# Moving the stores of the normalised tiles to GpSimd's queue, the shared weights' loads to a later place, and the transposes and half chunks around the last tile

## The chip, the cores and the metric

The kernel runs on one core of one Trainium2 chip. The metric is the device time of one execution in microseconds (us), taken as the median of three runs. The engines are named as in the profile: PE is TensorE (matmuls, with weight loads as PEld), DVE is VectorE, ACT is ScalarE, POOL is GpSimd, SP is SyncE. SP, ACT and POOL can each issue DMAs from a queue of their own. [...]

## The reference, cut to what matters

One transformer block with adaptive layer norm, over 2048 tokens of width 512, all in 32-bit floats: attention with 16 heads of 128, then a mixture of 64 experts of hidden size 128 with the best 4 per token, beside 2 shared experts of hidden size 512.

```python
h = _layernorm(x) * (1 + ca) + sa
x = x + ga * attention(h)                        # 16 heads, causal, output projection O_w
h = _layernorm(x) * (1 + cb) + sb
scores = softmax(h @ Wr + router_bias)           # 64 experts
topk_scores, topk_idx = top_k(scores, 4)
pos = running count of each expert's tokens      # valid where pos < 128
xb[eid, pos] = h[tok]
yb = (silu(xb @ Wg) * (xb @ Wu)) @ Wd            # each expert
out = sum over a token's 4 experts of w * yb
hs = silu(h @ Sg) * (h @ Su)                     # 2 shared experts
out = out + hs @ Sd
x = x + gb * out
```

## The kernel before

The tokens lie in 16 tiles of 128 rows, 4 tiles to a block of 512. The program has four stages. In all of them the order of the work is written out by hand (inside `manual_schedule`), by lists of closures and by tables that say behind which matmul of which tile something is emitted. Around these hand-written orders the compiler may still interleave the instructions of one stage with those of the next, where they are independent.

**Attention** (lines 188 to 670) ends with the last head's values. Its last lines store the attention of each head and pair of tiles to `atd` from GpSimd's queue (L489).

**Output projection with the router** (L873 to L938). For each tile `t` from 4 to 15, 16 matmuls (one for each head, index `hd`) of 128x512 build `pso` (L915) from the pair buffer `abs_[t // 2]`, which `load_ab` loads from `atd` on SP's queue (L544), and `wo`. At the end of a tile VectorE adds it to `acc` (L936) and `norm(t)` (L728 to L744) makes the normalised tile: statistics on VectorE, a square root on ScalarE (L735), then `h` on VectorE (L738, L741, L742), and a store of `h` to `h2d` in DRAM from SP's queue (L743). `h` has 4 buffers, so that `norm(t + 4)` needs the store of tile `t` to be finished. Tiles 0 to 3 were begun earlier and are finished at L899 to L908.

Between the 16 matmuls of a tile, four tables place the router's work of earlier tiles. The key is (tile, index of the matmul behind which it is emitted), the value is the tile or block concerned:

- `TURN`: `turn_h` transposes `h` of a tile on TensorE (`tp`, L749), and ScalarE copies it to `h2T` (L750).
- `LOGIT`: `logit` multiplies it with the router's weights (`pl`, L758). After every second tile `choose` (L766 to L807) follows on VectorE and ScalarE: softmax, best four, one-hot masks.
- `POSITION`: `positions` (L809 to L850) counts the seats on TensorE (`pos`, L819) and works out the seats on VectorE (L824 to L848). `pos` and `pl` share one PSUM bank.
- `SEAT`: `seat_tokens` (L852 to L871) collects the table of tokens per expert (L859). After the last block it gives `tok`, the list by which GpSimd gathers the experts' rows.

The loads of the next stage's shared weights, `wsg` and `wsu` (two of 1 MB each, L895 and L896), are issued on SP's queue at the head of this stage, behind the loads of `x`.

**Lead of the shared experts** (L1141 to L1178). `shared_up(b, i)` gives two half chunks: four matmuls with `wsg` and four with `wsu` (`psg`, L978), each of 128x512; after the second, `glu` makes `hs`: a sigmoid on ScalarE (L966) and two multiplications on VectorE (L967, L968). `psg` has three PSUM buffers. `LEAD = 8` half chunks are computed in this plain way, and the router's work of the last tile is placed between them, by their number `n`: the transpose of tile 15, its logits and `choose`, the positions and the seats of the last block. `wsd`, the shared experts' output weights, is loaded here (L1155) and multiplied by `gb` on GpSimd (L1157), eight instructions of 128x512. `token_sum` prepares sums of tokens on VectorE for the next stage.

**Experts and shared units** (L1183 to L1257). For every expert GpSimd gathers 128 rows of `h2d` by `tok` (L1190), TensorE transposes them (`tpx`, L1200) and runs the expert (`pse` L1207, `tph` L1222, `psy` L1228). `merge` interleaves this with the rest of the shared work. A shared unit does what two half chunks do with 7 products of half the size instead of 8 (Strassen's scheme: `first` to `fourth`, `pst`, L1062), that is 14 matmuls of 128x256, with sums on VectorE. `shared_down` (`psd`, L1122) multiplies `hs` by `wsd`. A **tail** (L1259 to L1299) gathers the experts' rows for every token, adds them and stores the result.

Of the kernel before, what the change touches and what calls it, by code (L numbers as in the profile page):

```python
# [18 lines left out]
P = 128  # L19
# [4 lines left out]
def adaln_block_kernel(  # L24
# [23 lines left out]
    nc = tc.nc  # L48
# [3 lines left out]
    S, _, HS = Sg.shape  # L52
# [5 lines left out]
    NHC = S * HS // P  # L58
# [3 lines left out]
    NP = NT // 2  # L62
# [15 lines left out]
    gb = const.tile([P, D], F32)  # L78
    atd = dram.tile([H, DH, N], F32)
    h2d = dram.tile([N, D], F32)  # L80
# [43 lines left out]
    with ExitStack() as att:  # L124
# [63 lines left out]
        with tc.tile_pool(name="pre", bufs=1) as pre, tc.manual_schedule():  # L188
# [4 lines left out]
            for b in range(NB):  # L193
                xb = pre.tile([P, 4, D], F32, name="xb", bufs=NB)
                nc.sync.dma_start(
                    out=xb, in_=x[0, b * 512 : (b + 1) * 512, :].rearrange("(i p) d -> p i d", p=P)
                )
                xs.append(xb)
                if b == 0:
                    wms = {}  # L200
                    for i in (1, 0):
                        wms[i] = pre.tile([P, DC, D], F32, name="wm", bufs=2)
                        nc.sync.dma_start(
                            out=wms[i],
# [334 lines left out]
        def load_ab(pr, dst=None, heads=((0, 4), (4, 8), (8, 12), (12, 15))):  # L539

            if pr not in abs_:
                abs_[pr] = vp.tile([P, H, 2 * P], F32, name="v") if dst is None else dst
            for a, b in heads:
                nc.sync.dma_start(  # L544
                    out=abs_[pr][:, a:b, :],
                    in_=atd[a:b, :, pr * 256 : (pr + 1) * 256].rearrange("h p t -> p h t"),
                )
# [130 lines left out]
    wsg = shw.tile([P, S, DC, HS], F32)  # L678
    wsu = shw.tile([P, S, DC, HS], F32)
# [48 lines left out]
    def norm(t):  # L728

        st = rt.tile([P, 6], F32, name="st", bufs=3)  # L730
        nc.vector.bn_stats(st, acc[:, t, :])
        mv = rt.tile([P, 2], F32, name="mv", bufs=3)
        nc.vector.bn_aggr(mv, st)
        rstd = rt.tile([P, 1], F32, name="rstd", bufs=3)
        nc.scalar.activation(rstd, mv[:, 1:2], AF.Sqrt, bias=eps, scale=1.0)  # L735
        nc.vector.reciprocal(rstd, rstd)
        h = rt.tile([P, D], F32, name="h", bufs=4)
        nc.vector.tensor_scalar(  # L738
            h, acc[:, t, :], mv[:, 0:1], rstd, ALU.subtract, ALU.mult
        )  # L740
        nc.vector.tensor_mul(h, h, cb)  # L741
        nc.vector.tensor_add(h, h, sb)  # L742
        nc.sync.dma_start(out=h2d[t * P : (t + 1) * P, :], in_=h)  # L743
        hs_[t] = h  # L744

    def turn_h(t):
# [131 lines left out]
    POSITION = {(5, 14): 0, (6, 10): 1}  # L878
    SEAT = {(6, 5): 0, (7, 0): 1}
    for t in range(7, NT):  # L880
        TURN[t, 7] = t - 1
        LOGIT[t, 12] = t - 1
        if t - 2 in LASTS:
            POSITION[t, 7] = LASTS.index(t - 2)
        if t - 3 in LASTS and t > 7:
            SEAT[t, 3] = LASTS.index(t - 3)
    with tc.manual_schedule():
        load_x(1)
        load_ab(3, heads=ALL)
        load_ab(2, heads=((15, 16),))  # L890
        route_consts()
        for j in range(2, NB):
            load_x(j)
        for s in range(S):
            nc.sync.dma_start(out=wsg[:, s], in_=Sg[s].rearrange("(k p) h -> p k h", p=P))  # L895
            nc.sync.dma_start(out=wsu[:, s], in_=Su[s].rearrange("(k p) h -> p k h", p=P))  # L896
        for t in range(NE):
            ps = psO.tile([P, D], F32, name="pso", tag="y")
            nc.tensor.matmul(  # L899
                out=ps,  # L900
                lhsT=last3[:, t * P : (t + 1) * P] if t < NE - 1 else ones,
                rhs=wo[:, H - 1, :],
                start=True,
                stop=True,
            )
            nc.vector.tensor_add(acc[:, t, :], parts[t], ps)
        for t in range(NE):
            norm(t)  # L908
        for t in range(NE, NT):
            pr, i = divmod(t, 2)  # L910
            if i == 0 and 3 <= pr < NP - 1:
                load_ab(pr + 1, heads=ALL)
            ps = psO.tile([P, D], F32, name="pso", tag="y")
            for hd in range(H):
                nc.tensor.matmul(  # L915
                    out=ps,
                    lhsT=abs_[pr][:, hd, i * P : (i + 1) * P],
                    rhs=wo[:, hd, :],
                    start=(hd == 0),
                    stop=(hd == H - 1),  # L920
                )
                if hd == 5:
                    nc.vector.tensor_add(acc[:, t, :], acc[:, t, :], ga)
                if (t, hd) in TURN:
                    turn_h(TURN[t, hd])
                if (t, hd) in POSITION:
                    positions(POSITION[t, hd])
                if (t, hd) in SEAT:
                    seat_tokens(SEAT[t, hd])
                if (t, hd) in LOGIT:  # L930
                    u = LOGIT[t, hd]
                    logit(u)
                    if u in LASTS:
                        for _ in choose(LASTS.index(u)):
                            pass
            nc.vector.tensor_add(acc[:, t, :], acc[:, t, :], ps)  # L936
            norm(t)
# [3 lines left out]
    with ExitStack() as ex:  # L941
# [154 lines left out]

        def fourth(n):
            u = units[n]
            (p2,) = products(n, (2,))
            nc.vector.tensor_add(u["g"][:, :HB], u["p1"], p2)  # L1100
            sig = sgp.tile([P, 512], F32, name="sig512")
            nc.scalar.activation(sig, u["g"], AF.Sigmoid)
            b, i = UNITS[n]
            hsh[b, i] = hsp.tile([P, 512], F32, name="hs")

            def finish():
                nc.vector.tensor_mul(sig, sig, u["g"])
                nc.vector.tensor_mul(hsh[b, i], sig, u["up"])

            glus.append(finish)  # L1110
            if b + 2 < NB:
                for j in {4: (1, 2), 5: (3,), 6: (4,)}.get(i, ()):
                    token_sum(b + 1, j)
            if n + 1 == len(UNITS):
                glus.pop()()
            del units[n]
# [17 lines left out]
            nc.sync.dma_start(out=out[0, t * P : (t + 1) * P, :], in_=acc[:, t, :])  # L1134


        LEAD = 8
        shared = []
        for i in range(LEAD // 2):
            shared += shared_up(0, i)  # L1140
# [12 lines left out]

        with tc.manual_schedule():
            nc.sync.dma_start(out=wsd, in_=Sd.rearrange("s (i p) d -> p (s i) d", p=P))  # L1155
            for i in range(NHC):
                nc.gpsimd.tensor_mul(wsd[:, i, :], wsd[:, i, :], gb)  # L1157
            for e in range(3):
                load_up(e)
                load_down(e)  # L1160
            for n, (_, f) in enumerate(shared[:LEAD]):
                f()
                if n == 0:
                    turn_h(NT - 1)
                if n == 1:
                    seat_tokens(len(BLOCKS) - 2)
                if n == 1:
                    logit(NT - 1)
                    choice = choose(len(BLOCKS) - 1)
                    next(choice)  # L1170
                if n == 2:
                    next(choice)
                if n == 4:
                    positions(len(BLOCKS) - 1)
                if n == 6:
                    seat_tokens(len(BLOCKS) - 1)
                if n >= 4:
                    token_sum(0, n - 3)  # L1178
        rts.close()
        tsp = ex.enter_context(tc.tile_pool(name="tsp", bufs=1))  # L1180
        wsp = ex.enter_context(tc.tile_pool(name="wsp", bufs=1))
# [163 lines left out]
```

## Time and profile before

| what | us |
|---|---|
| runs of the kernel before | 2517.18, 2517.94, 2519.73 |
| their median | 2517.94 |
| the profiled execution, device time | 2528.37 |
| its span in the trace | 2526.5 |
| TensorE busy in that span | 2427.2 |
| output projection and router, about | 1772 to 1983 |
| lead of the shared experts, about | 1983 to 2021 |
| experts and shared units, about | 2021 to 2400 |
| tail, about | 2400 to 2527 |

The profile is of one execution, and its times are counted from the start of the span. A line of the timeline has the start, the duration, the engine, the line of the kernel, the operation, what is written and read, the shapes and the count; a bracket at its end gives how long the engine had been idle before it, and what released it. Matmuls overlap, so their durations count some time twice: the distance between starts is what a group costs. A 32-bit matmul of 128x512 has two records in the trace. The granted clock of TensorE is given as a share of the full clock. A wait for several things is put down to the one that came last.

### The profile page before, as it was taken

To read this page: it belongs to the slowest core of one execution; us is meant where nothing else is said; L and a number is where in the kernel's file an instruction comes from. 1 tells how busy PE (TensorE), PEld (TensorE's weight loads), DVE (VectorE), ACT (ScalarE), POOL (GpSimd) and SP (SyncE) were. 2 spreads that over 40 slices of the span, in tenths; PEclk is the share of its full clock that TensorE was granted. 3 is DMA by queue.
4 is the path that set the end of the run, shared out by engine and by line. 5 is a ranking of instruction groups with operands and counts; after the bars stand their busy time and mean duration, and the time that the engine had idled before them with its cause. 6 is when DMAs were issued, how large, how long until landed. Compare 5 with 4: busy or idle time off the path is not lost.

```text
span 2526.5 us, 26293 instructions
## 1 busy us (share of the span) xinstructions
PE 2427.2 (96%) x8537; PEld 1529.5 (61%) x8537; DVE 1518.9 (60%) x2969; ACT 655.7 (26%) x1476; POOL 250.9 (10%) x306
## 2 busy tenths in 40 slices
PE   7999999999999999999999999979999899999989
PEld 4666666666666666666666666545444486877733
DVE  4566666666666666666666666664655552654645
ACT  3223323333333332323333223311111121222200
POOL 0000000000000000000000000040000211111173
PEclk9999999999999999999999999989999999999999
DMA  4234434444454444443444444574612376877564
GB/s 138 61 92 105 116 91 108 111 99 110 96 122 105 101 119 101 98 118 89 110 111 104 110 99 113 130 215 133 215 54 75 92 208 209 247 219 232 176 202 127
DMA packets 225423, 326.25 MB, mean 129 GB/s; under 512 B 32100, under 2 KB 140680, under 8 KB 225288
## 3 DMA queue, kind: packets, MB, share of 16 engines
q1 hardware_dynamic: 197960, 251.16, 38.5%
q0 software_dynamic: 18112, 56.64, 7.5%
q10 hardware_dynamic: 9216, 16.78, 1.8%
q8 instruction: 69, 1.13, 0.2%
q14 instruction: 66, 0.54, 0.1%
HBM read 139.91 MB, written 41.94 MB: 72 GB/s over the span
## 4 chain that ended last, share of the span: by engine, by line
PE 64%; DVE 19%; SPq 6%; issue 4%; DMA 4%; ACT 2%; another core or an unknown queue 0%; DVEq 0%; ACTq 0%; POOL 0%; POOLq 0%
PE pqk L169 12%; PE ps L408 11%; PE po L479 9%; DVE pt L461 7%; SPq L451 6%; PE pv L329 5%; PE pst L1062 5%; PE pso L915 4%; PE psd L1122 4%; PE pse L1207 4%; DVE nm L421 4%; DMA pt<-p 3%; PE psg L978 3%; DVE p L397 3%; PE psy L1228 2%
## 5 line engine op out<-in xcount | busy, mean ns | idle before, releaser
L427 ACT ACTIVATE p<-ps,nm 128x1024 f32<-128x1024 f32 (+7 forms) x384 | 331.9, 864 | 1042.3 <-DVE nm L425 369.7
L408 PE MATMUL ps<-kt,qt 128*128 128x512 f32 (+3 forms) x1280 | 535.7, 535 | 45.8 <-ACT p L427 45.0
L479 PE MATMUL po<-pt,v 128*128 128x256 f32 (+1 forms) x2304 | 567.0, 368 | 6.5 <-DVE pt L461 3.6
L479 PEld LDWEIGHTS po<-pt,v 128*128 128x128 f32 x2304 | 425.7, 190 | 221.0 <-issue 156.1
L421 DVE TENSOR_REDUCE nm<-ps 128x1 f32<-128x1024 f32 (+7 forms) x384 | 349.6, 910 | 91.2 <-PE ps L408 82.4
L461 DVE STREAM_TRANSPOSE pt<-pt 128x1664 f32<-128x1664 f32 (+2 forms) x160 | 318.0, 1988 | 66.2 <-DMA pt<-p 61.6
L408 PEld LDWEIGHTS ps<-kt,qt 128*128 128x128 f32 x1280 | 235.4, 191 | 196.7 <-issue 127.1
L420 DVE TENSOR_TENSOR ps<-ps,causal 128x128 f32<-128x128 f32 x256 | 74.4, 291 | 347.7 <-PE ps L408 347.7
L489 POOL DMA_DIRECT2D atd<-at x128 | 78.2, 612 | 1650.7 <-ACT at L488 1626.2
L329 PE MATMUL pv<-wv,hT 128*128 128x256 f32 x1024 | 240.3, 379 | 0.0
L169 PE MATMUL pqk<-hT,wk 128*128 128x512 f32 x512 | 233.0, 598 | 0.0
L169 PE MATMUL pqk<-hT,wq 128*128 128x512 f32 x512 | 230.0, 592 | 0.0
L397 DVE TENSOR_SCALAR p<-p,rs 128x1024 f32<-128x1024 f32 (+7 forms) x384 | 221.7, 605 | 9.3 <-DMA p<-atd 0.2
L329 PEld LDWEIGHTS pv<-wv,hT 128*128 128x128 f32 x1024 | 194.5, 190 | 31.4 <-issue 1.9
L915 PE MATMUL pso<-hT,v 128*128 128x512 f32 x384 | 175.6, 604 | 0.0
L169 PEld LDWEIGHTS pqk<-hT,wk 128*128 128x128 f32 x512 | 98.2, 192 | 103.3 <-issue 100.9
L169 PEld LDWEIGHTS pqk<-hT,wq 128*128 128x128 f32 x512 | 97.2, 190 | 96.4 <-issue 93.3
L1207 PE MATMUL pse<-wgu,xbT 128*128 128x256 f32 x512 | 121.1, 379 | 0.0
L915 PEld LDWEIGHTS pso<-hT,v 128*128 128x128 f32 x384 | 70.7, 192 | 74.5 <-issue 73.5
L1122 PE MATMUL psd<-wsd,hs 128*128 128x512 f32 x256 | 111.5, 592 | 0.0
L1207 PEld LDWEIGHTS pse<-wgu,xbT 128*128 128x128 f32 x512 | 94.0, 190 | 12.3 <-issue 1.4
L1190 POOL DMA_INDIRECT xb<-h2d,tok x64 | 65.0, 1016 | 293.9 <-PE tpx L1200 279.9
(263 smaller groups left out, 1956.7 us busy)
## 6 DMA issues: line engine op xcount, KB each, us to landing
pt<-p SPq DMA_DIRECT2D x768, 104.0 KB
pt<-p SPq DMA_DIRECT2D x256, 124.0 KB
pt<-p SPq DMA_DIRECT2D x256, 108.0 KB
atd<-at POOLq DMA_DIRECT2D x128, 128.0 KB
wgu<-in_L_ffn_Wg_dram SPq DMA_DIRECT2D x64, 256.0 KB
wgu<-in_L_ffn_Wu_dram SPq DMA_DIRECT2D x64, 256.0 KB
wd<-in_L_ffn_Wd_dram SPq DMA_DIRECT2D x64, 256.0 KB
ybd<-y ACTq DMA_DIRECT2D x64, 256.0 KB
```

The lines of the kernel that those rows point to most:

```text
L169: nc.tensor.matmul(out=ps, lhsT=w[:, k, :], rhs=hT[:, k, j * 512 : (j + 1) * 512], start=(k == 0), stop=(k == DC - 1),)
L329: nc.tensor.matmul(out=ps, lhsT=hT[:, k, t * P : (t + 1) * P], rhs=wv[:, k].rearrange("p i d -> p (i d)"), start=(k == 0), stop=(k == DC - 1),
L397: nc.vector.tensor_scalar(cols[:, :, a:b], cols[:, :, a:b], rs[:, n : n + 1], None, ALU.mult)
L408: nc.tensor.matmul(out=ps[:, o : o + wo], lhsT=q, rhs=kts[hd, (c0 + o) // 512][:, :wo], start=True, stop=True,)
L421: nc.vector.tensor_reduce(nm[:, n : n + 1], ps[:, :w], AX.X, ALU.max, negate=True)
L427: nc.scalar.activation(rows[:, r0 + c0 // P : r0 + (c0 + w) // P], ps[:, :w].rearrange("q (r b k) -> q r b k", b=4, k=32), AF.Exp, bias=nm ...
L451: nc.sync.dma_start(out=pt[32 * b : 32 * (b + 1), a * w : (a + 1) * w], in_=pb[32 * a : 32 * (a + 1), b * w : (b + 1) * w],)
L461: nc.vector.transpose(part, part)
L479: nc.tensor.matmul(out=po if wide else po[:, P:], lhsT=vts[g][:, kt, hh * DH : (hh + 1) * DH], rhs=rows[:, r : r + last + 1 : last] if wid ...
L915: nc.tensor.matmul(out=ps, lhsT=abs_[pr][:, hd, i * P : (i + 1) * P], rhs=wo[:, hd, :], start=(hd == 0), stop=(hd == H - 1),)
L1122: nc.tensor.matmul(out=ps, lhsT=hsh[b, f][:, i * P : (i + 1) * P], rhs=wsd[:, f, :], start=(f == 0), stop=(f == NHC - 1),)
L1207: nc.tensor.matmul(out=ps, lhsT=xts[e][:, k, :], rhs=weights[e][:, k].rearrange("p i h -> p (i h)"), start=(k == 0), stop=(k == DC - 1),)
```

## The change

It has five parts. The store of the normalised tile goes from SP's queue to GpSimd's. The loads of `wsg` and `wsu` go from the head of the output stage to tile 11 (the first shared expert) and tile 13 (the second), behind the load of the pair buffer. For tiles 7 to 15 the transpose of the tile before is emitted after matmul 10 instead of 7, and the logits after matmul 14 instead of 12. `LEAD` goes from 8 to 10 half chunks, and the work placed between the half chunks comes one half chunk later, so that one more half chunk stands ahead of the last tile's transpose and two follow the last seats. The multiplication of `wsd` by `gb` goes from GpSimd to VectorE, three instructions, three and two in the fourth step of the first three shared units; two of the later `token_sum` calls come one unit later.

```diff
@@ norm
-        nc.sync.dma_start(out=h2d[t * P : (t + 1) * P, :], in_=h)
+        nc.gpsimd.dma_start(out=h2d[t * P : (t + 1) * P, :], in_=h)
@@ tables
     for t in range(7, NT):
-        TURN[t, 7] = t - 1
-        LOGIT[t, 12] = t - 1
+        TURN[t, 10] = t - 1
+        LOGIT[t, 14] = t - 1
@@ output stage
-        for s in range(S):
-            nc.sync.dma_start(out=wsg[:, s], in_=Sg[s].rearrange("(k p) h -> p k h", p=P))
-            nc.sync.dma_start(out=wsu[:, s], in_=Su[s].rearrange("(k p) h -> p k h", p=P))
...
             if i == 0 and 3 <= pr < NP - 1:
                 load_ab(pr + 1, heads=ALL)
+            if i == 1 and pr >= NP - 1 - S:
+                s = pr - (NP - 1 - S)
+                if s < S:
+                    nc.sync.dma_start(out=wsg[:, s], in_=Sg[s].rearrange("(k p) h -> p k h", p=P))
+                    nc.sync.dma_start(out=wsu[:, s], in_=Su[s].rearrange("(k p) h -> p k h", p=P))
@@ fourth
             u = units[n]
+            for f in range(3 * n, min(NHC, 3 * n + 3)):
+                nc.vector.tensor_mul(wsd[:, f, :], wsd[:, f, :], gb)
             (p2,) = products(n, (2,))
...
-                for j in {4: (1, 2), 5: (3,), 6: (4,)}.get(i, ()):
+                for j in {5: (1, 2), 6: (3, 4)}.get(i, ()):
                     token_sum(b + 1, j)
@@ lead
-        LEAD = 8
+        LEAD = 10
...
             nc.sync.dma_start(out=wsd, in_=Sd.rearrange("s (i p) d -> p (s i) d", p=P))
-            for i in range(NHC):
-                nc.gpsimd.tensor_mul(wsd[:, i, :], wsd[:, i, :], gb)
...
             for n, (_, f) in enumerate(shared[:LEAD]):
                 f()
-                if n == 0:
+                if n == 1:
                     turn_h(NT - 1)
-                if n == 1:
+                if n == 2:
                     seat_tokens(len(BLOCKS) - 2)
-                if n == 1:
+                if n == 2:
                     logit(NT - 1)
                     choice = choose(len(BLOCKS) - 1)
                     next(choice)
-                if n == 2:
+                if n == 3:
                     next(choice)
-                if n == 4:
+                if n == 5:
                     positions(len(BLOCKS) - 1)
-                if n == 6:
+                if n == 7:
                     seat_tokens(len(BLOCKS) - 1)
-                if n >= 4:
-                    token_sum(0, n - 3)
+                if 5 <= n < 9:
+                    token_sum(0, n - 4)
```

## The prediction

> **What bounds the kernel now.** I read the page first (engine shares, slices), then a table of windows, then TensorE's timeline between 1772 and 2021 us, then who held its stalls. Every time below is in us.
>
> ```profile
> PE 2427.2 (96%) x8537; PEld 1529.5 (61%) x8537; DVE 1518.9 (60%) x2969; ACT 655.7 (26%) x1476; POOL 250.9 (10%) x306
> ...
> PE   7999999999999999999999999979999899999989
> ```
>
> TensorE is busy 96% of the span, so a gain is either less TensorE work or one of its rare holes. The windows (columns: length, busy time and count of each engine, clock, DMA share, GB/s) say where the holes are:
>
> ```profile
> 1772.00:1803.00 31.00, 30.23 (x96) 14.90 (x95) 17.98 (x35) 5.35 (x10) 1.68 (x7) 1.00 0.93 315
> 1803.00:1848.00 45.00, 40.04 (x143) 20.30 (x142) 32.05 (x95) 7.95 (x13) 0.00 (x0) 0.92 0.25 87
> 1848.00:1983.00 135.00, 129.04 (x423) 63.77 (x422) 70.51 (x192) 18.67 (x29) 0.00 (x0) 1.00 0.19 64
> 1983.00:2021.00 38.00, 31.36 (x98) 14.94 (x97) 23.93 (x52) 7.43 (x10) 13.77 (x11) 0.95 0.46 138
> 2021.00:2400.00 379.00, 379.00 (x1652) 282.97 (x1651) 193.75 (x463) 86.88 (x232) 63.51 (x63) 1.00 0.72 215
> ```
>
> The expert stage (2021 to 2400) has no hole; the output projection with the router (1772 to 1983) and the hand-over (1983 to 2021) have them. TensorE's timeline names them; the bracket is the idle time and its releaser:
>
> ```profile
> 1802.87 4.46 PE L915 MATMUL pso<-hT,v 128*128 128x512 f32 x10
> 1809.85 1.13 PE L978 MATMUL psg<-h2T,wsg 128*128 128x512 f32 x2 [2.52 <-ACT h2T L750]
> 1812.08 0.26 PE L819 MATMUL pos<-mask,before 128*128 128x64 bf16 x2 [1.11 <-DVE mask L792]
> ...
> 1812.20 2.05 PE L915 MATMUL pso<-hT,v 128*128 128x512 f32 x2
> ...
> 1846.85 0.66 PE L749 MATMUL tp<-ident,h 128*128 128x128 f32 x4 [1.33 <-DVE h L742]
> ...
> 1879.42 0.63 PE L749 MATMUL tp<-ident,h 128*128 128x128 f32 x4 [1.49 <-DVE h L742]
> ...
> 1989.94 1.11 PE L749 MATMUL tp<-ident,h 128*128 128x128 f32 x4 [4.29 <-DVE h L742]
> 1990.85 4.69 PE L978 MATMUL psg<-h2T,wsu 128*128 128x512 f32 x8
> ...
> 2014.61 3.65 PE L978 MATMUL psg<-h2T,wsu 128*128 128x512 f32 x8
> 2020.61 1.94 PE L1200 MATMUL tpx<-ident,xb 128*128 128x128 f32 x8 [2.35 <-issue]
> ```
>
> One 128x512 matmul is two records here: ten records in 4.46 is 0.857 a matmul. After the longer stalls the same work runs at half rate (two records in 2.05 at 1812.20, eight in 4.69 at 1990.85). The stall at 1809.85 begins on VectorE and ends at a store:
>
> ```profile
> 1793.53 28.00 SPq L743 DMA_DIRECT2D h2d<-h  x6
> ```
> ```profile
> 1805.65 0.55 DVE L738 TENSOR_SCALAR h<-acc,mv,rstd 128x512 f32<-128x512 f32 x1 [11.21 <-DMA h2d<-h]
> ```
>
> SP issues the first h store only after the 4 MB of shared weights; it lands 12 later, norm(4) lacks its fourth-back h buffer until then, and the router's choose(0), ScalarE's exp and the copy of h2T queue behind it.
>
> [...] idle times of 2.35, 2.52 with 1.11, and 4.29 are followed by half rate, those of 1.3 to 1.5 are not. [...] the atd store issued at 1754.60 releases SP's dependent load at 1757.92. [...] the trace shows L784 at 1.71 beside L1157's multiplies, 0.69 elsewhere.
>
> **The change part by part.**
>
> *A, stores on GpSimd, weights later.* From 1802.87 to the restart at 1847.49 TensorE's work is 34 512-wide matmuls (29.1), four logits (3.4), three transposes (1.3), two tables (0.9) and three positions (0.4), 35.1 against 44.6 elapsed. Of the loss of 9.5, 1.5 is the transpose of tile 6 (part B); 8.0 is this stall with its slow clock. In the changed kernel h(0) is ready at 1781, [...] norm(4) asks at 1794.3. Either way the wait goes. Next late: VectorE. Replaying its order with the durations of before, mask(0) comes near 1801.3 and mask(1) just in time; logit(4) waits about 0.65 for positions(1), logit(2) about 0.1. Gain 8.0 - 0.8 = 7.2. GpSimd has nothing else queued then (220.9 idle before L1157), so 16 issues of about 0.6 (atd: 0.54) hide.
>
> *B, transposes at 10, logits at 14.* Five transposes (tiles 6, 8, 10, 12, 14) stall; with the pipeline overlap tile 6 costs 1.5, the others 1.65 each: 8.1. h(t) is ready 10.8 after the logits that start choose. Now 9 + 3 matmuls and a position (10.4) lie between, before it was 11 (9.4). So 0.65 stays at tile 8 and 0.1 at tile 6; at tiles 10, 12 and 14 the built order puts one early psg matmul (0.857) just before the transpose, and the stall is gone. Gain 7.35. That psg waits for wsg: loaded behind load_ab(6), 3.1 MB at 315 GB/s is about 10, plus 3 of issue, and TensorE arrives 25 after the buffer came free. Moving the logits by two costs nothing by itself: positions are due a tile later.
>
> *C, tile 15.* Before: 4.5 lost and 1.55 of slow clock (0.5 + 1.1), 6.05. Now five psg matmuls (4.3) lie between the last pso and the transpose, which alone would cover it. But the built order puts glu(0) inside norm(15): ScalarE loads the sigmoid table (1.28), sig (0.6), the sqrt table (1.28), then rstd; VectorE's hs, which waits for the last wsu matmul, stands before the reciprocal and h. After those five matmuls come hs 0.6, reciprocal 0.2, h 0.6, 0.7, 0.7: stall 3.0 to 3.2, most likely with one slow window (1.7). Gain 6.05 - 4.9 = 1.15; the ends are 0 and 5.8.
>
> *D, ten half chunks.* Before: 2.57 idle until xb lands and 1.6 slow (1.94 for about 1.04, 1.73 for 1.03). Two more halves, 6.86, now follow the last seat; tok plus 5.25 (2015.36 to 2020.61) is covered. The price: eight 512-wide matmuls (6.86) replace a unit of 14 256-wide ones (6.0), 0.86. Gain 3.3, down to 2.3 if the second gather is late.
>
> *E, wsd scaled on VectorE.* Eight of 0.69 (L741's row), 5.5, go between other work in the expert stage, where VectorE is busy 51% and TensorE's three pst banks leave some 6 for a 2.1 burst. I take 0, ends 0 and +5.5. Freeing GpSimd speeds choose(7) by about 2.8, off the path.
>
> *F, token_sum one unit later.* Same eight instructions, needed a unit later; 0.
>
> The built order between the last psy and the tail is the same, so the shift reaches the end. Sum: 7.2 + 7.35 + 1.15 + 3.3 = 19.0. Against the profiled execution, 2528.4 - 19.0 = 2509.4 (span 2526.5 to 2507.5). That execution is 10.4 above the median of the runs; nothing of the change is in that difference, so 2517.9 - 19.0 = 2498.9.
>
> **Rivals.**
> R1, half the gain: the early wait stays because GpSimd's store lands late (over 13 after issue, against the 3.3 of atd), or E is exposed. For it: window 1772 to 1803 runs the DMA engines at 0.93. 19.0 - 7.2 gives 2506.1; with E too, 2511.6.
> R2, more: the stall of C escapes the slow window (1.7), and psg hides tile 15 better; or the stalls of the tail, which is paced by GpSimd's gathers, shrink when fewer transfers collide. 2490 to 2494. Against: the built order fixes C.
> R3, no change: the gain is used up downstream, TensorE waiting in the tail (window 2440 to 2480 has 29 busy of 40) for gathers. Against: gathers start when the last expert's rows land, which moves along. 2513 to 2523.
> R4, slower: the early psg of tile 11 stands in TensorE's queue ahead of everything, and wsg is not there. It decides once wsg lands over 25 after load_ab(6) may start, and makes the kernel slower by more than 0.2% when it lands about 49 after it: 2498.9 + 24 = 2523. For it: this stretch moved only 64 GB/s, at which 3.1 MB take 48. Against: that was all it asked for; 315 GB/s flowed before 1803.
>
> **How the numbers follow.** About 0.2% (5 us) is what a measurement of this kernel tells from no change. Forecast 0.62 (2492 to 2506), R1 0.17, R2 0.10, R3 0.04, R4 0.07. Faster 0.62 + 0.17 + 0.10 = 0.89, same 0.04, slower 0.07. The range runs from R2's low end, 2490, to inside R1, 2510; what lies outside is R3, R4 and the rest of R1.
>
> **What would show it.** A: no idle over 1 on VectorE before h of tile 4, clock 1.00 in 1803 to 1848. B: tile 8's transpose waits about 0.5, tiles 10 to 14 nothing. C: a transpose of tile 15 waiting about 3 for h, then a slow window. D: tpx with no idle before it. E: TensorE full after it. The prediction fails if psg waits for wsg at tile 11, if h of tile 4 still waits for a store, or if the tail grows.

## The result and the profile after

| | us |
|---|---|
| changed kernel, runs | 2493.62, 2496.90, 2498.73, 2499.74 |
| their median | 2497.82 |
| kernel before beside it, median of 4 | 2517.57 |
| ratio | 0.992, 95% interval 0.9904 to 0.9936 |
| profiled execution of the changed kernel, device time | 2493.62 |
| its span | 2491.8 |

The kernel became 19.75 us faster; 2498.9 was forecast. The two profiled executions differ by more, 2526.5 against 2491.8 in the span, that is 34.7. Some 12 us of this are a stop near the end that a second profile of the kernel before does not have, as shown below.

The page of the changed kernel, TensorE's line of the busy times and its slices:

```profile
PE 2419.3 (97%) x8525; PEld 1526.6 (61%) x8525; DVE 1514.8 (61%) x2966; ACT 656.0 (26%) x1476; POOL 249.2 (10%) x314
...
PE   7999999999999999999999999979999999999999
```

TensorE's busy time fell by 7.9 only, mostly because matmuls at half clock had counted as busy (the mean granted clock is 0.990 before and 0.994 after). (The twelve records fewer save nothing: eight matmuls of 128x512 stand where fourteen of 128x256 were, which step D prices at 0.86 more.) The rest of the gain is idle time. The windows of the changed kernel, cut at the same stages as before (length, busy time and count of each engine, clock, DMA share, GB/s):

```profile
1772.00:1803.00 31.00, 30.77 (x95) 15.18 (x96) 24.23 (x54) 6.62 (x13) 4.03 (x11) 1.00 0.68 226
1803.00:1848.00 45.00, 45.00 (x176) 23.33 (x176) 32.82 (x94) 6.77 (x11) 1.62 (x3) 1.00 0.28 92
1848.00:1969.00 121.00, 120.69 (x392) 59.64 (x391) 62.45 (x172) 18.25 (x27) 3.78 (x7) 1.00 0.27 92
1969.00:2006.00 37.00, 34.02 (x108) 15.99 (x107) 21.61 (x53) 9.31 (x12) 3.68 (x4) 1.00 0.47 143
2006.00:2400.00 394.00, 394.00 (x1677) 287.00 (x1676) 205.26 (x475) 85.76 (x231) 80.50 (x79) 1.00 0.73 217
```

The second row is the one that step A was about: TensorE works all 45.00 us at full clock, where before it worked 40.04 at 0.92. No row of this table has a clock below 1.00. One hole is left, in the fourth row. TensorE's timeline names it, together with the transposes that stalled before:

```profile
1868.00 0.66 PE L749 MATMUL tp<-ident,h 128*128 128x128 f32 x4 [0.31 <-DVE h L742]
...
1898.92 1.02 PE L980 MATMUL psg<-h2T,wsg 128*128 128x512 f32 x2
1899.77 0.60 PE L749 MATMUL tp<-ident,h 128*128 128x128 f32 x4
...
1969.70 3.60 PE L980 MATMUL psg<-h2T,wsu 128*128 128x512 f32 x8
1976.28 0.63 PE L749 MATMUL tp<-ident,h 128*128 128x128 f32 x4 [2.98 <-DVE h L742]
1976.74 3.60 PE L980 MATMUL psg<-h2T,wsg 128*128 128x512 f32 x8
...
2006.34 1.04 PE L1202 MATMUL tpx<-ident,xb 128*128 128x128 f32 x8
```

Tile 8's transpose waits 0.31, tile 10's follows one early psg matmul with no wait (tiles 12 and 14 look the same), tile 15's waits 2.98, tpx does not wait. Early psg matmuls are those of the half chunks that stand ahead of tile 15's transpose, four in the kernel before and eight in the changed one; the built order can move them up into the output stage. Eight psg records in 3.60 right after the wait of 2.98 is full rate; before, after 4.29, they took 4.69. The h store now comes from GpSimd; the view of its instructions, and how long the stores took to land:

```profile
L743 POOL DMA_DIRECT2D h2d<-h x16: 540/540/582, 1780.5 to 1976.4; - x16
...
DMA to landing us min/median/max: 2.3/4.0/6.9
```

VectorE's h of tile 4 starts at 1793.58 with no idle time before it, where before it waited 11.21 for the store of tile 0. Behind that wait choose(0) stood too: its logits (L758) were through by 1796.95, its first instruction (L770) started at 1807.56.

### The profile page after: what moved, and what is told of

Its sections match the earlier page's. It is cut to its first block, busy times and chain, and to the rows that moved or that the text cites. A ratio compares the mean times of both kernels' runs of the same rounds, so it can differ in the third digit from the quotient of the medians.

```text
span 2491.8 us, 26256 instructions
## 1 busy us (share of the span) xinstructions
PE 2419.3 (97%) x8525; PEld 1526.6 (61%) x8525; DVE 1514.8 (61%) x2966; ACT 656.0 (26%) x1476; POOL 249.2 (10%) x314
## 4 chain that ended last, share of the span: by engine, by line
PE 67%; DVE 17%; SPq 6%; DMA 4%; issue 4%; ACT 1%; DVEq 0%; POOL 0%; ACTq 0%; POOLq 0%
PE pqk L169 12%; PE ps L408 12%; PE po L479 9%; DVE pt L461 7%; PE pso L917 6%; SPq L451 6%; PE pv L329 5%; PE pst L1064 5%; PE pse L1209 4%; PE psd L1126 4%; DVE nm L421 4%; DMA pt<-p 3%; PE psg L980 3%; DVE p L397 3%; PE psy L1230 2%
```

## The experiments

A yardstick for single stages is needed, since two executions of one kernel differ by several us elsewhere. I take the time from the first output matmul (pso of L896 or L899) to the first expert matmul (pse), the stretch that holds every edit but the scaling of wsd. In a kernel with ten half chunks the stretch holds 6.86 more, and the expert stage one unit of 6.0 less (both as in step D); so 6.0 is taken off its stretch, and the price of 0.86 stays in. The yardstick repeats well: the first profile of the kernel before gives 251.65, the second and third of the changed kernel 236.73 and 236.71.

| kernel | start to first pse | length | less 6.0 for ten half chunks | gain on 251.8 |
|---|---|---|---|---|
| before, second profile | 1772.15 to 2023.96 | 251.81 | 251.81 | |
| stores alone | 1775.24 to 2020.12 | 244.88 | 244.88 | 6.9 |
| weights later alone | 1774.35 to 2018.20 | 243.85 | 243.85 | 8.0 |
| transposes later alone | 1777.09 to 2021.40 | 244.31 | 244.31 | 7.5 |
| ten half chunks alone | 1775.44 to 2025.99 | 250.55 | 244.55 | 7.3 |
| changed kernel | 1772.23 to 2008.94 | 236.71 | 230.71 | 21.1 |
| changed, gating after tile 15 | 1776.35 to 2010.17 | 233.82 | 227.82 | 24.0 |
| changed, scaling on GpSimd again | 1777.73 to 2014.43 | 236.70 | 230.70 | 21.1 |
| changed, stores on SP again | 1773.04 to 2007.08 | 234.04 | 228.04 | 23.8 |
| changed, eight half chunks | 1773.70 to 2006.96 | 233.26 | 233.26 | 18.6 |
| changed, transposes early again | 1777.84 to 2023.72 | 245.88 | 239.88 | 11.9 |

### One part of the change at a time

Four kernels, each the kernel before with one part, on one chip, on which the kernel before took 2532.43.

Stores alone:

```diff
-        nc.sync.dma_start(out=h2d[t * P : (t + 1) * P, :], in_=h)
+        nc.gpsimd.dma_start(out=h2d[t * P : (t + 1) * P, :], in_=h)
```

> The kernel before with one edit: the store of h on GpSimd's queue; the weights' loads stay at the head of SP's queue. Theory of the record (a queue of its own is enough[...]): no wait of VectorE for a store at h of tile 4, no half-rate window near 1810, the stall of part A gone; the built order also puts one early psg before tile 6's transpose, so about 7 to 8 us faster, near 2510. Rival (the 4 MB of weights must leave, whatever the queue): VectorE still waits 5 us or more for the store at tile 4, and the time stays within 3 us of before. Tail rival (what the profile shows beyond the forecast sits in the tail): no gain here at all.

Measured: 2524.03, ratio 0.9973 (0.9964 to 0.9982), 8.4 less. The stall at tile 4 and its half-rate window are gone; the transposes wait 1.33 to 1.49 and tile 15 waits 4.29 as before. The next transpose behind the stall is tile 5's:

```profile
1820.93 0.60 PE L749 MATMUL tp<-ident,h 128*128 128x128 f32 x4
```

Counted from the first output matmul (1775.24) that is 45.69; in the second profile of the kernel before it is 53.84 (1825.99 - 1772.15), of which one early psg matmul takes 0.86. So the stall is worth 7.3.

Weights later alone (the loads of wsg and wsu moved to tiles 11 and 13):

```diff
-        for s in range(S):
-            nc.sync.dma_start(out=wsg[:, s], ...)
-            nc.sync.dma_start(out=wsu[:, s], ...)
...
+            if i == 1 and pr >= NP - 1 - S:
...
```

> The kernel before with one edit: the loads of wsg and wsu at tiles 11 and 13; the stores stay on SP's queue. Theory of the record: SP reaches the first store about 9 us earlier and only the loads of x are ahead of it, VectorE's wait at tile 4 is 0 to 2 us, part A's 7 us are gained, and the built order's early psg before the transposes of tiles 12 and 14 save 2 to 2.5 more: near 2508. Rival (the queue matters[...]): a wait of 5 us or more stays, 2514 to 2518. Tail rival: no gain.

Measured: 2522.33, ratio 0.9962 (0.9952 to 0.9972), 10.1 less. The stall at tile 4 is gone here too, with the stores still on SP. Tile 5's transpose:

```profile
1820.04 0.60 PE L749 MATMUL tp<-ident,h 128*128 128x128 f32 x4
```

From 1774.35 that is 45.69 again, and 45.69 in the changed kernel as well. So the two halves of step A are alternative cures of one stall, and either alone takes all of it away. The 6.9 and 8.0 of the table hold other things too: with the weights late, three early psg matmuls cover tile 12's transpose and one leaves tile 14 a wait of 0.61, while tile 6's wait grows to 2.18.

Transposes later alone:

```diff
-        TURN[t, 7] = t - 1
-        LOGIT[t, 12] = t - 1
+        TURN[t, 10] = t - 1
+        LOGIT[t, 14] = t - 1
```

> The kernel before with one edit: transposes at 10, logits at 14. Theory of the record (10.8 us from the logits to h, one matmul 0.857): the transposes of tiles 10, 12 and 14 wait 0.3 to 0.6 instead of 1.5, tile 6's next to nothing, tile 8's nothing because the built order has a psg before it; about 6 us faster, near 2511.5, and the stall of tile 4 with its slow window stays. Rival (moving the logits moves h along, so the wait only shifts): the transposes still wait 1.2 or more, time within 2 us of before. Tail rival: no gain.

Measured: 2523.62, ratio 0.9969 (0.9956 to 0.9981), 8.8 less, where some 6 were expected, and 7.5 in the stretch. Three waits of 0.30 to 0.31 at tiles 10, 12 and 14 are left; the stall at tile 4 stays with its slow clock, shorter by 0.7, which is in the 7.5.

Ten half chunks alone (LEAD, the lead's turns and the token sums as in the change):

```diff
-        LEAD = 8
+        LEAD = 10
```

> The kernel before with one edit: LEAD 10 with what lies between the half chunks one later. Theory of the record (price of D, and the built order decides C): no idle before the first tpx, but tile 15's transpose waits as long as before or longer, 4.3 to 6, since the built order takes all eight early psg matmuls into tiles 5 to 9 and leaves none to cover it, and glu(0) stands in norm(15); D gives 3.3, the early psg before tiles 6 and 8 give 3, the longer wait takes 1.5: near 2513. Rival (the half chunk covers tile 15 as the change means it to): that transpose waits under 1, and 2507 or less. Tail rival: no gain.

Measured: 2525.47, ratio 0.9979 (0.9970 to 0.9987), 7.0 less, where some 5 were expected. TensorE's timeline of this kernel:

```profile
1944.18 0.63 PE L749 MATMUL tp<-ident,h 128*128 128x128 f32 x4 [1.48 <-DVE h L742]
...
1991.18 1.12 PE L749 MATMUL tp<-ident,h 128*128 128x128 f32 x4 [5.85 <-DVE h L742]
...
2023.39 1.04 PE L1200 MATMUL tpx<-ident,xb 128*128 128x128 f32 x8
```

tpx no longer waits, as step D says, but tile 15 waits 5.85: all eight early psg matmuls were used up in tiles 5 to 9, none is left ahead of this transpose. Part of the gain comes from there, since the transposes of tiles 6 and 8 don't wait, and 2.8 from the stall at tile 4, which stays but brings no half-rate window here. So a part's effect alone is not its effect in the whole: the early psg matmuls go wherever the built order has room, and each edit moves them.

Still, the four gains in the stretch, with step A counted once, add up to 8.0 + 7.5 + 7.3 = 22.8, near the 21.1 of the whole. That is luck in part: the waits of tiles 6 and 8 and a part of the stall at tile 4 are counted twice in this sum, and the last of the three edits made tile 15 worse.

### Parts taken back out of the changed kernel

On a second chip (kernel before 2515.83) the changed kernel took 2500.45, ratio 0.9939 (0.9925 to 0.9952).

> The changed kernel as it is, timed and profiled once more on another chip, as the yardstick of the three runs beside it. Two things are open. First the stretch near the end (about 2440 to 2460 of the kernel before), in which TensorE, VectorE and ScalarE stand still for 8 to 14 us in the profiles of the kernel before and of the four single edits, and which the one profile of the changed kernel lacks. If the change removes that stop (rival R2 of the prediction, the tail shrinks), this profile lacks it too and the gain against the kernel before is about 30 us in every profile. If the stop comes by chance or belongs to the profiled execution alone, it is there or not with no regard to the change, and the timed gain stays near 20 us (ratio 0.991 to 0.993). Second the stretch from the first output projection to the first expert matmul: 236.7 us again, tile 15's transpose waiting 3.0 us for h with no half-rate window after it.

Its stretch is as in the first profile: tile 15 waits 2.98 and no half-rate window lies in it.

The gating of the first half chunk held back behind tile 15's transposes:

```diff
-                    hsh[b, i] = hsp.tile([P, 512], F32, name="hs")
-                    glu(hsh[b, i], parts[0], parts[1], 512)
+                    def close():
+                        hsh[b, i] = hsp.tile([P, 512], F32, name="hs")
+                        glu(hsh[b, i], parts[0], parts[1], 512)
+
+                    if (b, i) == (0, 0):
+                        held.append(close)
+                    else:
+                        close()
...
                     turn_h(NT - 1)
+                    held.pop()()
```

> The changed kernel with one edit: the gating of the first half chunk of the shared expert (sigmoid table, sig, hs) is held back until tile 15's transposes are issued, so that norm(15) does not queue behind it. My reading of step C says that the 2.98 us wait of tile 15's transpose comes from these instructions alone: it falls to below 0.5 us and the kernel is 2.5 to 3 us faster than the changed one (ratio to before about 0.991, if the changed one has 0.992). Rival: h of tile 15 is late because of VectorE's own norm (bn_stats to the last add, about 4.5 us after the last output projection), and the wait stays above 2 us. Second rival: the wait moves on, to the psg banks that the held gating frees later or to the gather before tpx, and the time does not change.

Measured: 2496.63, ratio 0.992 (0.9906 to 0.9934), 3.8 less than the changed kernel beside it. What it removes is seen first in the changed kernel, in the timeline of ScalarE and VectorE around norm(15):

```profile
1969.93 1.28 ACT L968 ACT_TABLE_LOAD   x1 [5.49 <-PE psg L980]
...
1971.22 0.60 ACT L968 ACTIVATE sig<-psg 128x512 f32<-128x512 f32 x1
...
1971.84 1.28 ACT L735 ACT_TABLE_LOAD   x1
...
1973.13 0.29 ACT L735 ACTIVATE rstd<-mv,eps 128x1 f32<-128x1 f32 x1
1973.33 0.69 DVE L970 TENSOR_TENSOR hs<-sig,psg 128x512 f32<-128x512 f32 x1 [0.79 <-PE psg L980]
...
1973.94 0.15 DVE L736 RECIPROCAL rstd<-rstd 128x1 f32<-128x1 f32 x1
```

VectorE's statistics are done at 1970.67, but the square root is done only at 1973.42, since two table loads and the sigmoid stand before it. Each table load takes 1.28; sig starts 0.01 after its load ends, and the next load 0.02 after sig. Then hs, which waits for the last psg matmul, stands ahead of the reciprocal: that starts at 1973.94, 0.52 after the root is done, where with the gating held back it is 0.04 (1975.12 to 1975.16). In that run TensorE's timeline reads

```profile
1973.82 3.60 PE L982 MATMUL psg<-h2T,wsu 128*128 128x512 f32 x8
1977.50 0.63 PE L749 MATMUL tp<-ident,h 128*128 128x128 f32 x4
1977.97 3.60 PE L982 MATMUL psg<-h2T,wsg 128*128 128x512 f32 x8
```

and the stretch is 2.9 shorter, what the wait of 2.98 was worth. Both rivals fall: VectorE's own norm is covered by the five psg matmuls, and nothing comes late in place of the wait.

The scaling of wsd back on GpSimd:

```diff
-            for f in range(3 * n, min(NHC, 3 * n + 3)):
-                nc.vector.tensor_mul(wsd[:, f, :], wsd[:, f, :], gb)
...
+            for i in range(NHC):
+                nc.gpsimd.tensor_mul(wsd[:, i, :], wsd[:, i, :], gb)
```

> The changed kernel with the scaling of wsd put back on GpSimd, where it was before. Step E says that the eight multiplies on VectorE cost nothing, because VectorE is busy 51% in the expert stage: then this kernel has the changed one's time within 1 us. Rival (the upper end of step E): they are exposed in full, 8 x 0.69 = 5.5 us, and this kernel is faster than the changed one by up to 5.5 us. [...]

Measured: 2500.18, ratio 0.9931 (0.9918 to 0.9945), 0.3 less than the changed kernel beside it, and a stretch of 236.70 against 236.71. From the first pse to the end it takes 483.97; three profiles of the changed kernel have 482.65 to 483.62. Step E shows no cost, and an exposure of 5.5 is excluded.

The stores of h back on SP, the weights still late:

```diff
-        nc.gpsimd.dma_start(out=h2d[t * P : (t + 1) * P, :], in_=h)
+        nc.sync.dma_start(out=h2d[t * P : (t + 1) * P, :], in_=h)
```

> The changed kernel with the stores of h back on SP's queue, the weights still loaded late. Loading the weights late took the stall at tile 4 away by itself (the run with that edit alone had none), so step A should lose nothing there. What is left is order: this kernel's early psg matmuls stand at tile 13, two of them and two more at tile 15, so the transposes of tiles 10 and 12 should wait about 0.3 to 0.7 us again (1 us in all), and the gating of the first half chunk stands after norm(15), which should take the 3 us wait of tile 15 away. Sum: 2 us faster than the changed kernel to equal. Rival: a store on SP queues behind load_ab(6), load_ab(7) and the 4 MB of weights from tile 11 on, h buffers come back 10 us late once, and the kernel is 3 to 8 us slower than the changed one.

Measured: 2495.96, ratio 0.9919 (0.9906 to 0.9933), 4.5 less than the changed kernel, more than the 2 expected; the stretch is 2.7 shorter. The built order puts one early psg matmul ahead of the transposes of tiles 12 and 14 each, six ahead of tile 15's, and the gating behind norm(15). TensorE's timeline at tile 15:

```profile
1969.30 1.88 PE L980 MATMUL psg<-h2T,wsg 128*128 128x512 f32 x4
1971.01 3.60 PE L980 MATMUL psg<-h2T,wsu 128*128 128x512 f32 x8
1974.44 0.60 PE L749 MATMUL tp<-ident,h 128*128 128x128 f32 x4
```

No wait at all, and two waits of 0.30 at tiles 8 and 10. No store was late: the slowest landed 9.1 after its issue, and no h on VectorE waited for one. The stores' way to GpSimd thus gains nothing once the weights are late; by moving the built order it costs the wait of tile 15. These two kernels, gating held back and stores on SP, beat both the kernel before and the changed kernel: their runs (2491.82 to 2498.27 and 2492.91 to 2496.14) lie below all five of the changed kernel beside them (2499.25 to 2502.58). Between the two there is no difference to be told.

### What the profiles' other difference was, and two parts undone

On a third chip the kernel before and the changed kernel were profiled side by side, with two runs that each take one part back.

> The kernel before as it is, profiled once more on the chip that also runs the changed kernel beside it. Theory that the stop of 8 to 14 us near 2450 belongs to the chip or the occasion: on a chip where the kernel before takes about 2516 its profile has no stop there, and the two profiles then differ by the 1772-to-tail stretch alone, about 21 us, give or take the clock of the attention part. Rival, the change removes the stop: it is there (over 5 us without work on TensorE, VectorE and ScalarE, near 2440 to 2460) although the changed kernel beside it has none.

> The changed kernel as it is, the yardstick of the two undo runs beside it: tile 15's transpose waits 2.98 us, no half-rate window between 1750 and 2480, no stop near 2450. If that stop comes with the chip and not with the kernel, it is in both profiles or in neither.

Measured: before 2517.37, changed 2498.34, ratio of the changed 0.9913 (0.9897 to 0.9928). The first profile of the kernel before, in windows, has this near its end:

```profile
2446.00:2456.00 10.00, 2.67 (x7) 0.89 (x5) 0.47 (x1) 0.00 (x0) 7.56 (x9) 0.89 0.72 213
```

TensorE, VectorE and ScalarE nearly stand still for 10 us while GpSimd and the DMAs go on. The second profile of the same kernel has in its tail

```profile
2440.00:2450.00 10.00, 10.00 (x25) 4.47 (x24) 6.88 (x10) 1.05 (x2) 7.72 (x8) 1.00 0.84 263
```

and no such stop; from the first pse to the end it takes 489.94 against 501.73. So the stop does not belong to the kernel before as such, and that the first profile of the changed kernel lacks it is no gain of the change. The four single edits all had it on the chip where the kernel before took 2532; the two later chips never showed it. No profile of the changed kernel was taken on that chip, so whether it would have the stop there is not shown. What stops three engines at once the trace does not name (the releasers it gives are "issue" and "remote"), and this stays open.

With this second profile the spans differ by 2513.9 - 2491.8 = 22.1, of which 21.1 is the stretch and 1.1 the tail, where psg's wait for sig is 1.7 before and 0.7 after (0.5 to 1.8 in other profiles with ten half chunks, so this is no sure gain of the change).

Eight half chunks again:

```diff
-        LEAD = 10
+        LEAD = 8
```

> The changed kernel with step D undone: eight half chunks ahead of the last tile's gather, the shared loop's turns and token sums as before. In the built order this leaves one psg matmul ahead of each transpose of tiles 10, 12, 14 and 15, and the gating of the first half chunk after norm(15). By step D tpx waits about 2.4 us for its gather again with a half-rate window, less one cheaper unit: +3.3 us. By my reading of the wait at tile 15 it is worse there than in the changed kernel, since one psg matmul instead of five stands before the transpose: 3.4 to 4.3 us of wait instead of 2.98, with a half-rate window (another 1.7) if such a wait brings one. So 4 to 6.5 us slower than the changed kernel. Rival: the tenth half chunk only pays for itself (the gather's latency is hidden anyway once the stage is tighter), within 1.5 us.

Measured: 2499.87, ratio 0.9926 (0.9911 to 0.9942), 1.5 more than the changed kernel; the stretch is 2.5 longer. By time alone this could be the rival, since the runs of the two kernels overlap; the waits speak against it. TensorE's timeline:

```profile
1970.30 1.02 PE L980 MATMUL psg<-h2T,wsg 128*128 128x512 f32 x2
1974.84 0.63 PE L749 MATMUL tp<-ident,h 128*128 128x128 f32 x4 [3.52 <-DVE h L742]
...
2003.56 0.63 PE L1202 MATMUL tpx<-ident,xb 128*128 128x128 f32 x4 [1.93 <-DMA xb<-h2d,tok]
2004.74 0.65 PE L1202 MATMUL tpx<-ident,xb 128*128 128x128 f32 x4 [0.55 <-DMA xb<-h2d,tok]
```

The waits are those expected, 0.54 more at tile 15 and 2.48 at tpx, less 0.86 for the cheaper unit. No half-rate window follows either of them, and this is where 4 to 6.5 was too much.

Transposes at 7 and logits at 12 again:

```diff
-        TURN[t, 10] = t - 1
-        LOGIT[t, 14] = t - 1
+        TURN[t, 7] = t - 1
+        LOGIT[t, 12] = t - 1
```

> The changed kernel with step B undone: transposes at 7 and logits at 12 again. In the built order the early psg matmuls then stand before tiles 10 (three), 12 (three) and 14 (two), so these transposes are still covered; only tiles 6 and 8 wait 1.5 us each, 2.7 us more than in the changed kernel. But all eight early psg matmuls are used up by then, so tile 15's transpose waits 5.5 to 6 us, as it did with the lead alone, instead of 2.98, with a long half-rate window (3.4 us lost). Sum: 8 to 9 us slower than the changed kernel; the gain of 7.35 that step B names comes back at tile 15 rather than at tiles 10 to 14. Rival 1, the step as written: 7.35 us slower with waits of 1.5 us at all five transposes. Rival 2: only the 2.7 us of tiles 6 and 8.

Measured: 2505.80, ratio 0.9949 (0.9932 to 0.9966), 7.5 more than the changed kernel; the stretch is 9.2 longer. TensorE's timeline:

```profile
1841.81 0.66 PE L749 MATMUL tp<-ident,h 128*128 128x128 f32 x4 [2.18 <-DVE h L742]
...
1874.38 0.63 PE L749 MATMUL tp<-ident,h 128*128 128x128 f32 x4 [1.49 <-DVE h L742]
...
1939.56 1.88 PE L980 MATMUL psg<-h2T,wsu 128*128 128x512 f32 x4
1941.27 0.60 PE L749 MATMUL tp<-ident,h 128*128 128x128 f32 x4
...
1988.30 1.12 PE L749 MATMUL tp<-ident,h 128*128 128x128 f32 x4 [5.86 <-DVE h L742]
```

Tiles 10 to 14 stay covered, by psg matmuls; the price is paid at tiles 6 and 8 and at tile 15, whose wait grows from 2.98 to 5.86 and is followed by two half-rate windows. The window from 1987.30 on:

```profile
1987.30:1994.10 6.80, 5.80 (x10) 2.93 (x11) 0.91 (x2) 0.59 (x1) 0.54 (x1) 0.52 1.09 356
```

## Why the prediction was right

The forecast gain was 19.0. Measured were 19.75, 15.4 and 19.1 on three chips, and 21.1 in the stretch plus 1.1 in the tail between two profiles without the stop. By the steps, counted from the first output matmul, with 0.857 taken off for each psg matmul that stands ahead (second profile before, first profile of the changed kernel):

| start of | before | changed | gain |
|---|---|---|---|
| tile 5's transpose | 52.98 | 45.69 | 7.3 |
| tile 15's transpose | 213.38 | 197.19 | 16.2 |
| first tpx | 220.19 | 199.83 | 20.4 |
| first pse | 224.39 | 202.43 | 22.0 |

The lines of the kernel before, second profile, and of the changed kernel that the table starts from and that are not shown above:

```profile
1825.99 0.60 PE L749 MATMUL tp<-ident,h 128*128 128x128 f32 x4
...
1988.96 1.12 PE L749 MATMUL tp<-ident,h 128*128 128x128 f32 x4 [4.29 <-DVE h L742]
...
2019.76 1.94 PE L1200 MATMUL tpx<-ident,xb 128*128 128x128 f32 x8 [2.38 <-issue]
```
```profile
1817.92 0.60 PE L749 MATMUL tp<-ident,h 128*128 128x128 f32 x4
```

The 22.0 less the price of 0.86 is the 21.1. It splits into A 7.3, B 7.6, C 2.9 and D 3.3, where 7.2, 7.35, 1.15 and 3.3 were forecast.

**A, 7.2.** Confirmed: no idle time of VectorE before h of tile 4, the clock 1.00 from 1803 to 1848, as the prediction's list of signs had it. But the size is right by two errors that cancel. The loss of 8.0 was too large: with the stores alone, the matmuls that the prediction adds up to 35.1 take, with tile 6's wait, 37.35 (1804.98 to 1842.33), where 35.1 and 1.5 make 36.6; so of the 44.6 the stall is 7.3. And the 0.8 that VectorE was to cost next did not show: no wait of TensorE is left in this window. Either of the two edits was enough, which the prediction did not say: it treats them as one. For the store of 256 KB from GpSimd the author's estimate was about 10 at the most, from h(0) at 1781 until the loads ahead are through near 1791 at 315 GB/s; how short it could be was an estimate with no trace behind it. The trace of the changed kernel has 2.3 at the least, 4.0 in the median and 6.9 at the most, all of them in time for norm(4), which was to ask at 1794.3. The store to atd that the prediction names, 3.3 from its issue to the load that waits for it (1754.60 to 1757.92), moves 128 KB, half of that, and so says little of it. GpSimd's 16 issues take 0.54 each, as taken from atd.

**B, 7.35.** Confirmed. From tile 5's to tile 15's transpose 8.9 are gained, of which 1.3 is tile 15's own wait (4.29 to 2.98); 7.6 is left for B. In the changed kernel tile 8 waits 0.31 where 0.65 was forecast, tile 6 and tiles 10 to 14 nothing. R4's point, that the early psg of tile 11 could wait for wsg, is answered by the trace: the first wsg load is issued at 1875.9, takes 10.3, and psg asks at 1898.92, some 12.7 later.

**C, 1.15.** The mis-sized term. The wait was forecast at 3.0 to 3.2 and is 2.98, for the reason given, as the run with the gating held back shows. But it was to come "most likely with one slow window (1.7)", and none came in any of the four profiles with this wait. So the step brings 1.3 from the wait and, by the prediction's own count, 1.6 from the slow clock of before, 2.9 instead of 1.15. That is R2's first mechanism. Why none came is read from the traces in the last section: it goes with where the wait falls, which the prediction had no hold on.

**D, 3.3.** tpx follows its predecessor without idle time. From tile 15's transpose to the first pse 5.8 are gained; less the 1.6 of C and the price of 0.86 that is 3.3. Undone alone the step costs 2.5 in the stretch, 0.54 of it at tile 15. The term counted 1.6 of slow clock after the wait of before, which the second profile of the kernel before has too; in the undo run that wait, now 1.93 and 0.55, brings no slow window, so seen from there the two half chunks are worth less than forecast.

**E and F, 0.** E was tested and shows no cost. F was not tried by itself.

**The sum.** The mechanisms account for 21.1 and not 19.0, and C is most of the difference. That the medians came out at 19.75 and 19.1 is luck in part, for an execution also carries the slow windows of the attention part, which the change does not touch. On the third chip the two profiles differ by 22.4 from the first output matmul on, but by 15.5 in all, since the changed kernel's reached that matmul 6.9 later. Whether this is why the medians gain less than the 22 of the profiles is not shown.

**The difference of 10.4** between the profiled execution and the runs was said to hold nothing of the change. The stop near 2450, 11.8 long, lies in it: the second profiled execution, without the stop, took 2515.74, like the runs. So the sum made against the profile could be carried to the median.

R1 falls: the slowest store took 6.9, below the 13 at which it begins, and E is not exposed. R3 falls: from the first pse to the end the changed kernel takes 482.86, the kernel before 489.94, and the unit moved ahead accounts for 6.0 of it (with eight half chunks again it is 488.94). The tail neither grows nor, as R2 had it, shrinks by more than about 1.

## What to carry over

Where a hand-written order leaves spare matmuls (here eight psg) that can go anywhere, they cover whichever stall the built order puts them before, so the worth of an edit has to be read from where they end up: the late transposes were worth 7.5 alone and 9.2 when taken back, at other tiles each time. An activation that needs another table, slipped in front of a short square root, and the multiplication behind it, slipped in front of the reciprocal, together held up a tile's norm by 3 us: what stands in ScalarE's queue between the statistics and their root is worth a look in the trace. And before a profile's difference is explained, profile the old kernel a second time: 11.8 of the 34.7 us here belonged to one execution and not to the kernel.

## What was not expected of the hardware

In the traces here half-rate windows begin on a grid. In the record of the granted clock of the kernel before, those near 1812, 1990 and 2020 start 177.5 and then 30.7 apart, 52 and 9 times 3.41, and each window lasts 3.41 or a whole multiple of it, but for the one that the end of the span cuts off. The length of a wait alone tells little. Of waits for h, 4.29, 4.38, 5.85 and 5.86 were followed by slow windows each time, 2.98 (four profiles) and 3.52 (one) never; of waits at tpx, 2.12 with 0.57 and 2.35 to 2.40 were, 1.93 with 0.55 was not.

What sorts nearly every case is the share of one grid window that is idle. Lay the grid where the clock record has it and count as idle what lies between matmul records (their ends are modelled, so a share is good to a few hundredths). Then in all 14 profiles, from 40 to 2480, every window at full clock that was idle for 0.59 or more was followed by a slow one, 91 of them, and none that was idle for 0.53 or less; in between 3 were followed and 14 not. The wait of 2.38 before tpx in the second profile before fills 0.64 of one window. The 2.98 of the changed kernel is cut in two, 0.41 and 0.46, and with the scaling back on GpSimd 0.58 and 0.29. By this count it was where the wait fell that spared C its slow window; a later start of the same wait could have put 0.87 into one window. This is read from the traces; no run moved a wait to test it.

Slow windows also lengthen stages that the change doesn't touch, in one execution more than in another. The attention part, the same instructions in all these kernels, ended between 1772.15 and 1779.04. In the window 1728 to 1732 the third profile of the changed kernel (the one beside the second profile of the kernel before) reads

```profile
1728.00:1732.00 4.00, 3.19 (x5) 1.55 (x6) 2.74 (x3) 1.64 (x4) 0.00 (x0) 0.61 1.00 319
```

and the second profile of the kernel before reads

```profile
1728.00:1732.00 4.00, 4.00 (x15) 2.35 (x14) 2.74 (x3) 1.09 (x2) 0.00 (x0) 1.00 0.05 19
```

with a clock of 0.61 in the one and 1.00 in the other. This profile of the changed kernel has four such windows more than the other in the attention part (near 238, 1610, 1661 and 1729). Each loses half of 3.41, together 6.8, which is the difference of the starts, 1779.04 - 1772.15 = 6.9.
